# Layer 1 of a two-layer model: TensorE's steps put in another order by ranks and a re-measured planner clock

## The chip, the core and the metric

The kernel runs on one core of a Trainium2 chip. The metric is the device time of the whole program in microseconds; the kernel before has a median of 4030.48 us over three runs. TensorE is PE in the profile (PEld is its weight load), VectorE is DVE, ScalarE is ACT, GpSimd is POOL, and SyncE, which issues most transfers, is SP.

## The reference

The program computes two layers on x of shape (8, 1024, 256), all in float32. Layer 0 (attention, two expert layers and a Fourier block) is untouched here. Layer 1, cut to what matters:

```python
x = x + hla(layernorm(x), Wq, Wk, Wv, Wo)          # linear attention of higher order, 16 heads of 32, a scan over 1024 tokens
x = x + tanh(layernorm(x) @ W @ A1 @ A2 + bias)    # "ffn"
x = x + window(layernorm(x), Wqkv, bqkv, Wout, bout)  # softmax attention in windows of 128, 16 heads of 16
x = x + tanh(layernorm(x) @ W @ A1 @ A2 + bias)    # the same ffn

# one step of the scan in hla, G = 0.99
C_prev = G * C_QV
Gm   = G * Gm  + k[:, None] * (k @ C_prev)[None, :]
S_K  = G * S_K + k[:, None] * k[None, :]
C_QV = C_prev  + q[:, None] * v[None, :]
o    = q @ (S_K @ C_QV - Gm)
```

## The kernel before

Layer 1 handles a sequence (b, 0 to 7) in four pairs (i) of two chunks of 128 tokens; a chunk is c in the linear part and n in the window part. The scan is done by chunks: products of a chunk's queries and keys are masked and multiplied by tables of powers of 0.99, and a state of three 32x32 matrices a head passes from chunk to chunk.

The work is written as ten generators, each one a chain of steps that may interleave with the others:

- `enter` loads a pair of x (`x<-xb` on SP), eight pairs being resident at most.
- `linear_rows` ("lrows"): layernorm and transposes of a pair (helper `normed`, L1167), projections qt and kt (L1303), v (L1325), the masked products sk and sp (helper `head_products`, L1231 on PE, L1237 on DVE) and the transposes kw, dk, dq (L1343, L1358).
- `linear_chain` ("lchain"): the recurrence of a chunk: wt (L1251 and L1263), its transposes (L1392), ut, the new state (L1422, L1431, DVE L1440, POOL L1446), the products sr (L1231).
- `linear_out` ("lout"): the chunk's output (L1251, L1263), the projection with Wo (L1484) and the addition to x.
- `ffn` twice ("lffn" and "wffn"): layernorm, transposes, one product with the three matrices multiplied beforehand (L1189, L1198), tanh on ACT, addition on POOL (L1210).
- `window_rows` ("wrows"): layernorm, transposes, projections of k (L1510), q (L1530) and v (L1555, L1564), and on POOL the differences vd (L1582).
- `window_scores` ("wscores"): four banks of scores (L1599), the corner select and row maximum on DVE (L1613, L1615), exponentials on ACT (L1620).
- `window_columns` ("wcol"): transposes of the exponentials (L1641), copied by ACT (L1645) and, masked, by DVE (L1646).
- `window_out` ("wout"): products with v and vd (L1669), the denominators transposed (L1686, copied by ACT at L1692), the division on DVE (L1696), the projection (L1704).

A generator yields `step(cost, needs, acc, slots, tiles, dve)` before each piece of TensorE work. The class `Turns` keeps a planner's clock in units of about 0.108 us (a step of cost 16 is eight matmuls of 128x256, and takes 1.73 us in the trace). `ready` is the time at which the step's events and buffers are there by that clock; `run` takes the step with the earliest time and writes its instructions. TensorE executes in exactly that written order (`manual_schedule(engines={PE})`); DVE, ACT and POOL each have an in-order queue too, but the framework sorts theirs from the program as written. `use(engine, after, cost)` advances an engine's clock:

```python
start = max(self.engines[engine], after + 1.4)
self.engines[engine] = start + cost - 0.85
return start + cost + 0.6
```

and in `run` the choice among ready steps is

```python
change = 0.85 if request["tiles"][0] not in (None, self.tiles) else 0.0
start = at + change
if not self.ranks and self.engines["DVE"] < self.now + 15.0:
    change -= 0.05 * request["dve"]
key = (at + (0.0 if self.ranks else change), self.ranks.get(group, self.share.get(group, 0.0)), i)
```

`tiles` is how the step splits the 128x128 array: "whole", "rows" (four tiles of 32 rows), "columns" (four of 32 columns) or "halves". `self.ranks` is filled for layer 0 alone. PSUM has eight banks ("acc"); a bank is free again when the last reader of its step is done.

## Time and profile before

| what | value |
|---|---|
| median of 3 runs | 4030.48 us (4027.52 to 4034.27) |
| the profiled execution: its own time | 4030.48 us |
| the profiled execution: span, first to last instruction | 4028.5 us |
| mean granted TensorE clock | 0.974 of full speed |
| TensorE busy over the span | 3794.1 us (94%) |
| DVE, ACT, POOL busy over the span | 60%, 37%, 25% |
| layer 1, from 1687 us to the end | 2341.5 us, of which PE is busy 2223.93 us |

The busy time of PE is modelled, since its matmuls are pipelined; start times are recorded. All 31776 matmul records that layer 1 should have are in the trace, so that each can be assigned to the step that wrote it. Layer 1 has 1808 steps with TensorE work.

### The profile page before, as it was taken

The numbers are of one execution on the slowest core, as the hardware profiler recorded it, in microseconds if no ns is written. First come the engines' busy times: TensorE is split into PE (matmuls) and PEld (weight loads), VectorE is DVE, ScalarE is ACT, GpSimd is POOL, SyncE is SP. The second block draws the span as 40 slices with busy tenths as digits, with TensorE's granted clock in tenths as the row PEclk, the third lists the DMA queues.
The fourth block names the chain that finished last, engine by engine and source line by source line (L and its number), as shares of the span: only waits on it lengthen the run. The fifth ranks groups of instructions, "written<-read, shape, count | busy, mean of one in ns | idle before, by whom it ended". The sixth has DMA issues, their size and how long they took to land.

```text
span 4028.5 us, 92928 instructions
## 1 busy us (share of the span) xinstructions
PE 3794.1 (94%) x39176; PEld 2873.4 (71%) x39176; DVE 2409.9 (60%) x5653; ACT 1475.6 (37%) x4279; POOL 987.8 (25%) x1068
## 2 busy tenths in 40 slices
PE   8998999998699999999999999999999999999997
PEld 5665666676466666677778777777787777887775
DVE  5698036547765710156766666766766666667566
ACT  2322225322333212133534534434443445335335
POOL 1104463523242463211111111111211111111111
PEclk9998999999899999999999999999999999999999
DMA  4224444424243554200000000000000000000000
GB/s 137 85 69 142 114 122 107 107 69 121 65 106 86 134 130 108 58 2 7 7 12 7 13 7 7 12 7 7 12 7 12 7 7 12 13 5 5 7 5 9
DMA packets 164112, 196.43 MB, mean 49 GB/s; under 512 B 11248, under 2 KB 141296, under 8 KB 163696
## 3 DMA queue, kind: packets, MB, share of 16 engines
q1 hardware_dynamic: 139120, 156.92, 13.0%
q0 software_dynamic: 24576, 33.57, 5.0%
q8 instruction: 309, 5.06, 0.5%
q14 instruction: 107, 0.88, 0.1%
HBM read 131.60 MB, written 58.85 MB: 47 GB/s over the span
## 4 chain that ended last, share of the span: by engine, by line
PE 68%; DVE 15%; ACT 7%; issue 5%; POOL 4%; DMA 1%; SPq 0%; POOLq 0%; ACTq 0%; DVEq 0%
PE acc L489 10%; PE acc L517 9%; PE acc L1303 5%; PE acc L1263 5%; PE acc L1251 4%; PE acc L1231 4%; ACT w_ex L1620 3%; PE acc L1599 3%; PE acc L1484 2%; PE acc L1198 2%; PE acc L1669 2%; PE acc L1325 2%; DVE ln_st L270 2%; POOL ln_rs L273 2%; PE acc L595 2%
## 5 line engine op out<-in xcount | busy, mean ns | idle before, releaser
L273 POOL TENSOR_TENSOR ln_rs<-ln_rs,nhalf 128x2 f32<-128x2 f32 (+1 forms) x192 | 160.3, 836 | 1311.6 <-DVE ln_rs L272 1240.2
L489 PE MATMUL acc<-xgt,w1e 128*128 128x512 f32 x1024 | 460.1, 600 | 0.0
L1620 ACT ACTIVATE w_ex<-acc,w_nm 128x128 f32<-128x128 f32 x1024 | 362.8, 385 | 246.5 <-DVE w_nm L1615 240.6
L517 PE MATMUL acc<-w2e,ht 128*128 128x256 f32 x2048 | 452.3, 380 | 0.0
L517 PEld LDWEIGHTS acc<-w2e,ht 128*128 128x128 f32 x2048 | 385.6, 190 | 56.4 <-issue 5.9
L497 ACT ACTIVATE ht<-acc,b 128x512 f32<-128x512 f32 x256 | 174.2, 687 | 556.1 <-PE acc L489 555.8
L489 PEld LDWEIGHTS acc<-xgt,w1e 128*128 128x128 f32 x1024 | 192.9, 192 | 217.4 <-issue 212.0
L1303 PE MATMUL acc<-l_xt,hw 128*128 128x256 f32 x1024 | 240.0, 384 | 1.4 <-ACT l_xt L1174 0.8
L525 DVE SCALAR_TENSOR_TENSOR y<-acc,gate,gb 128x256 f32<-128x256 f32 x128 | 61.1, 478 | 293.5 <-PE acc L517 239.4
L270 DVE BATCH_NORM_STATS2 ln_st<-x 128x6 f32<-128x256 f32 x512 | 198.9, 409 | 55.6 <-POOL x L1210 36.1
L275 DVE TENSOR_SCALAR xn<-x,ln_mv,ln_rs 128x256 f32<-128x256 f32 x384 | 149.7, 434 | 137.7 <-POOL ln_rs L273 137.4
L1613 DVE COPY_PREDICATED acc<-consts,acc 128x256 f32<-128x256 int32 x512 | 193.0, 422 | 63.6 <-PE acc L1599 53.0
L1620 ACT ACTIVATION_READ_ACCUMULATOR w_ex<-acc,w_nm 128x1 f32 x1024 | 229.0, 224 | 0.0
L1446 POOL COPY state_bd<-state 32x384 f32<-32x384 f32 x224 | 112.6, 503 | 438.1 <-DVE state L1440 395.6
L1303 PEld LDWEIGHTS acc<-l_xt,hw 128*128 128x128 f32 x1024 | 191.2, 192 | 30.4 <-issue 2.4
L1646 DVE TENSOR_TENSOR w_pt<-acc,consts 128x512 f32<-128x512 f32 x256 | 167.1, 685 | 73.1 <-ACT w_pt L1645 71.3
L1237 DVE TENSOR_TENSOR sr<-acc,consts 128x512 f32<-128x512 f32 x256 | 158.9, 682 | 83.0 <-PE acc L1231 83.0
L512 POOL TENSOR_SCALAR gb<-b,gate 128x256 f32<-128x256 f32 x128 | 195.5, 1528 | 7.6 <-DVE index L433 7.5
L1615 DVE TENSOR_REDUCE w_nm<-acc 128x2 f32<-128x256 f32 x512 | 191.8, 416 | 0.0
L1237 DVE TENSOR_TENSOR sp<-acc,consts 128x512 f32<-128x512 f32 x256 | 158.7, 682 | 51.9 <-PE acc L1231 51.6
L1237 DVE TENSOR_TENSOR sk<-acc,consts 128x512 f32<-128x512 f32 x256 | 158.6, 682 | 37.3 <-PE acc L1231 37.3
L1645 ACT COPY w_pt<-acc 128x512 f32<-128x512 f32 x256 | 145.6, 620 | 94.0 <-PE acc L1641 82.9
(241 smaller groups left out, 7904.9 us busy)
## 6 DMA issues: line engine op xcount, KB each, us to landing
w1e<-in_W_dram SPq DMA_DIRECT2D x64, 512.0 KB
w2e<-in_W_dram SPq DMA_DIRECT2D x64, 512.0 KB
x<-in_x_dram SPq DMA_DIRECT2D x16, 512.0 KB
xa<-x SPq DMA_DIRECT2D x16, 512.0 KB
xna<-t_xn SPq DMA_DIRECT2D x16, 512.0 KB
x<-xa SPq DMA_DIRECT2D x16, 512.0 KB
gb<-g SPq DMA_DIRECT2D x32, 256.0 KB
xb<-x SPq DMA_DIRECT2D x16, 512.0 KB
```

What stands on the lines that cost most here:

```text
L270: nc.vector.bn_stats(st[:, i, :], src[:, i, :])
L273: nc.gpsimd.tensor_tensor(rs[:, :n], rs[:, :n], nhalf[:, :n], ALU.pow)
L489: nc.tensor.matmul(ps, w1e[:, k, (f % 4) * P : (f % 4 + 1) * P], xgt[:, k, :], start=k == 0, stop=k == 1,)
L497: nc.scalar.activation(h, ps, AF.Gelu_apprx_tanh, bias=b1[:, e * NT + f : e * NT + f + 1])
L512: nc.gpsimd.tensor_scalar(gb, r["b2", e], gate, None, ALU.mult)
L517: nc.tensor.matmul(ps[:, :D], ht[f][:, j * P : (j + 1) * P], r["w", e][2 + f // 4][:, f % 4, :], start=f == 0, stop=f == F // P - 1,)
L1237: nc.vector.tensor_tensor(dst, ps.rearrange("p (g t) -> p g t", t=P), bc4(const(mask)), ALU.mult)
L1263: nc.tensor.matmul(ps[32 * h : 32 * h + 32, g * P : (g + 1) * P], lhs(g, h), rhs[h][:, g, :], start=fresh and g == 0, stop=i == len(cols) - 1,
L1303: nc.tensor.matmul(ps[:, gi * 256 : (gi + 1) * 256], hw[:, k, g * 384 + col : g * 384 + col + P], xt[:, k, :], start=k == 0, stop=k == 1,)
L1613: nc.vector.copy_predicated(sc[:, :, 0, :], below, sc[:, :, 1, :])
L1615: nc.vector.tensor_reduce(nm, sc[:, :, 0, :], AX.X, ALU.max, negate=True)
L1620: nc.scalar.activation(ex[:, 2 * (j % 2) + e, :], sc[:, e, 0, :], AF.Exp, bias=nm[:, e : e + 1], accum_out=den[:, m, j, e : e + 1],)
```

## The change

No instruction of the computation is added or taken away; the planner's arithmetic is changed, and with it the order in which layer 1's steps are written. (1) Each step gets a `rank`, a number of units added to its key, so that it counts as later or, where negative, as earlier. (2) Leaving a "rows" step costs 2.1 units in the clock rather than 0.85. (3) The hand-over from TensorE to another engine costs 1.85 rather than 1.4 units (`use`), and between other engines 0 rather than 1.4 (`then`). (4) A few costs differ: POOL's power in the layernorm 7 rather than 10, a scores step 8 rather than 9, and vd counts from the end of the v additions. The core of the diff:

```diff
-    def use(self, engine, after, cost):
-        start = max(self.engines[engine], after + 1.4)
+    def use(self, engine, after, cost, lag=1.4):
+        start = max(self.engines[engine], after + lag)
         self.engines[engine] = start + cost - 0.85
         return start + cost + 0.6
...
-                    change = 0.85 if request["tiles"][0] not in (None, self.tiles) else 0.0
+                    change = 0.0
+                    if request["tiles"][0] not in (None, self.tiles):
+                        change = 2.1 if self.tiles in ("rows", "small") else 0.85
                     start = at + change
-                    if not self.ranks and self.engines["DVE"] < self.now + 15.0:
-                        change -= 0.05 * request["dve"]
+                    if not self.ranks:
+                        change += request["rank"]
+                        if self.engines["DVE"] < self.now + 15.0:
+                            change -= 0.05 * request["dve"]
...
-            done, use = turns.done, turns.use
+            done = turns.done
+            def use(engine, after, cost):
+                return turns.use(engine, after, cost, 1.85)
+            def then(engine, after, cost):
+                return turns.use(engine, after, cost, 0.0)
...  normed: layernorm and transposes
-                t = use("DVE", turns.now, 9.5)
-                t = use("POOL", t, 10)
-                done[tag, key, "n"] = use("DVE", t, 7)
-                t = yield step(4, [(tag, key, "n")], acc=1, slots=(tag,))
+                t = then("DVE", turns.now, 9.5)
+                t = then("POOL", t, 7)
+                done[tag, key, "n"] = then("DVE", t, 7)
+                t = yield step(4, [(tag, key, "n")], acc=1, slots=(tag,), rank=-1)
...
-                            t = yield step(9, needs, acc=4, slots=("w_ex", "w_ex"), dve=25)
+                            t = yield step(8, needs, acc=4, slots=("w_ex", "w_ex"), dve=25, rank=1)
...
-                                t_max = use("DVE", use("DVE", t, 4) - 1.4, 4)
+                                t_max = then("DVE", use("DVE", t, 4) - 1.4, 4)
...
-                        t = use("DVE", t, 4)
-                    acc_until(t)
+                        end = use("DVE", t, 4)
+                    acc_until(end)
...
-                            t = done["vd", b, m - 1] = use("POOL", t, 11)
+                            t = done["vd", b, m - 1] = then("POOL", end, 10)
```

The ranks, in units: `enter` 1; qt and kt 2; sk -11; dq -34; transposes of wt -2; ut -2; state -1; sr -2; projection with Wo 2; window k 5, q -29, v -64; scores 1; denominators -1; window projection 7; transposes of a layernorm -1; all other steps 0. The step with the smallest key is taken next. Its place on the clock is still `at` plus the real change of tiles, so that a rank alters the choice and not the lengths that the clock counts.

## The prediction

> **What bounds the kernel now.** I read the page first, then the stages by windows, then the timeline around single waits.

> ```profile
> span 4028.5 us, 92928 instructions
> PE 3794.1 (94%) x39176; PEld 2873.4 (71%) x39176; DVE 2409.9 (60%) x5653; ACT 1475.6 (37%) x4279; POOL 987.8 (25%) x1068
> ```

> TensorE sets the time; no other engine comes near. By windows, layer 1 is 2341.5 us, evenly loaded in the middle (a period of 577 us, two sequences) and thinner at its ends:

> ```profile
> core 0: us, PE busy (x) PEld busy (x) DVE busy (x) ACT busy (x) POOL busy (x), PEclk, DMA share, GB/s
> 1687.00:1787.00 100.00, 93.59 (x1333) 75.51 (x1337) 52.60 (x114) 32.25 (x80) 12.32 (x19) 0.93 0.04 14
> ...
> 2364.00:2941.00 577.00, 553.22 (x7950) 445.72 (x7952) 378.31 (x901) 249.46 (x831) 96.65 (x128) 0.98 0.03 9
> ...
> 3884.00:4028.50 144.50, 121.46 (x1478) 89.68 (x1476) 88.67 (x221) 65.32 (x242) 22.66 (x25) 0.94 0.03 9
> ```

> In the middle PE is idle for only 23.8 of 577 us. Busy time hides more, so I took start to start from the timeline, step by step. A kind of step has a usual length (the tenth percentile: a transpose of four blocks 0.44 us, a projection L1303 1.73, scores 1.08, a "rows" product 1.10). Over layer 1 the usual lengths make some 2042 of 2334.5 us, the half clock takes 45, and waits some 247. Two hundred and forty-seven is all that an order can win. A typical wait:

> ```profile
> 2673.00 1.16 PE L1251 MATMUL acc<-kt,state_bd 128*128 128x128 f32 x8
> 2674.09 1.08 PE L1263 MATMUL acc<-sk,v 128*32 128x128 f32 x32
> 2675.10 1.09 PE L1641 MATMUL acc<-consts,w_ex 128*128 128x128 f32 x8
> 2678.63 0.63 PE L1392 MATMUL acc<-consts,wt 128*128 128x128 f32 x4 [2.44 <-DVE sp L1237]
> ```

> ```profile
> 2675.40 1.25 DVE L272 TENSOR_SCALAR ln_rs<-ln_mv 128x2 f32<-128x2 f32 x1
> 2677.47 0.41 DVE L275 TENSOR_SCALAR xn<-x,ln_mv,ln_rs 128x256 f32<-128x256 f32 x1 [0.82 <-POOL ln_rs L273]
> 2677.80 2.48 DVE L1237 TENSOR_TENSOR sp<-acc,consts 128x512 f32<-128x512 f32 x4
> ```

> L1392 needs a PSUM bank that sp frees; sp stood behind a layernorm that waited for POOL. Three short steps stood between sp's products and L1392: too little work to cover the hand-over. Such waits are spread over many lines: by my count the scores take 41 us, L1641 25, L1669 20, the sk products 19, the sr products 19.

> **The change part by part.**

> *Instructions.* None is added. Comparing the built programs, layer 0 is identical on every engine, and layer 1 has the same first steps; PE's order differs from 1742.6 us on. SP's order is the same throughout, so every load and store keeps its place in that queue. A load now runs some 203 us of TensorE work ahead of its layernorm in the steady part, 290 before: far above the few us for which DVE waited on `x<-xb` (4.1 us in all). I cost the loads at nothing; were the lead gone, 24 later pairs would pay at most the 5 us that the planner itself allows. POOL's work moves with its steps and is within the counts below; it is busy 97 of 577 us. Semaphore waits change by some tens an engine; I cost them at nothing, since each is tied to a hand-over counted below.

> *Changes of tiling.* By how the array is really split (a scores step is a row step too), PE changes it 902 times before and 864 times after; leaving rows goes from 309 to 313. In the trace a step that is followed by another tiling is about 0.1 us longer (L1303 1.82 rather than 1.73; L1641 0.53 rather than 0.44). 38 fewer x 0.1 = -4 us. [...] I take -4.

> *Waits.* No trace shows the new order, so I bound it. For each waiting step I took the last TensorE step that must be over first, followed through the order of the DVE, ACT and POOL queues too, and summed the usual lengths between the two: the cover. Beside it stands the wait that this trace shows at such cover:

> | cover, us | steps before | mean wait before | steps after |
> |---|---|---|---|
> | under 0.5 | 43 | 1.15 | 7 |
> | 0.5 to 1 | 56 | 0.70 | 72 |
> | 1 to 1.5 | 107 | 0.28 | 59 |
> | 1.5 to 2 | 191 | 0.16 | 124 |
> | 2 to 3 | 278 | 0.16 | 262 |
> | 3 to 5 | 637 | 0.06 | 641 |
> | over 5 | 391 | 0.035 | 556 |

> Means times counts give 244 us before and 193 after: -50, the cautious end, since steps of unequal need share a row. The same table by kind of waiting step: -67. What is missing to a cover of 3 us sums to 779 us before and 540 after (-31%), to 2 us to 268 and 164 (-39%); of 247 that is -77 and -96. At the other end I took for each kind of hand-over the shortest lag seen (fifth percentile) and counted only what is missing to that: 436 places and 231 us before, 244 places and 102 us after: -129. There the transposes of the exponentials fall from 53 us in 27 places to 10 in 8, the window's first layernorm behind tanh and POOL's addition from 29 to 4, and vd (POOL L1582) from 12 to none. I take -90, between the last two and above the cautious end because the gains lie where lags are long.

> What comes late next: the Wo projection (L1484) behind the denominators' transposes (L1686), at 28 places with 1.1 us of cover for ACT's copy L1692; wt's transposes behind ACT's copy, 1.0 at some 30 places; sr behind ut on DVE, about 1.7 at 37. Those stay as waits and are in the counts.

> *Clock.* The windows view at three places of one period:

> ```profile
> core 0: us, PE busy (x) PEld busy (x) DVE busy (x) ACT busy (x) POOL busy (x), PEclk, DMA share, GB/s
> ...
> 2021.60:2028.40 6.80, 5.30 (x37) 4.01 (x40) 1.54 (x3) 3.70 (x12) 0.64 (x1) 0.51 0.01 2
> 2233.30:2240.10 6.80, 5.90 (x20) 4.25 (x18) 4.30 (x10) 2.22 (x4) 1.27 (x1) 0.51 0.00 0
> 2274.20:2281.00 6.80, 5.78 (x62) 4.85 (x62) 6.39 (x15) 2.91 (x16) 0.00 (x0) 0.51 0.01 2
> ```

> Each is 6.8 us at half clock, 3.4 us lost, and each follows a cluster of waits (before 2233.3 the four scattered starts of L1231, 3.0 us longer than usual). [...] The trace has them after waits in every period, so by the rows up to 31 us (three in each 577 us, and some more) could go. Between 0 and -31 I take -10: some clusters go, new ones may come.

> *End.* After the last linear projection 82.7 us of TensorE work remain, 71.3 before; at that end PE is idle 16% against 4% in the middle. 11.4 x 0.12 = +1.4, say +2.

> **Sum.** -4 - 90 - 10 + 2 = -102 us. The profiled execution took 4030.48 us (span 4028.5, 2.0 around it), which is also the median of the three runs: 4030.5 - 102 = 3928.5.

> **The rivals.**

> *A. Half the gain.* Queues of DVE and ACT add what the covers don't show: the cautious -50, no clock back, -4 and +2: 3978. For it: 72 steps in the row 0.5 to 1, more than before. Against: the counts follow those queues' order.

> *B. The waits only move.* The new order takes away covers that now work by luck; 247 us of waits remain, and -4 of tilings and +2 of the end give 4028, within measurement of no change. This is also the case in which the change does not do what it says: the planner's clock still errs by more than its ranks win. Against it: every row of the cover table under 0.5 and from 1 to 2 us is thinner.

> *C. Slower: ACT's copy of the denominators.* One mechanism, at one place: the Wo projection now follows L1686 at 28 places and needs the bank that L1692 frees on ACT, with 1.1 us of cover. On ACT a scores step is eight exponentials and eight reads (362.8 + 229.0 us over 128 steps = 4.6 us). If the copy stands behind a whole such block, each place waits about 4.6 + 0.9 - 1.1 = 4.4 us, 28 x 4.4 = 123 us, against a gain of 102: 4051. It decides from 102 / 28 = 3.6 us a place. For it: in the built ACT queue exponentials and two copies w_pt stand just ahead of the copy. Against: they belong to a step some 7 us earlier in PE's order and are mostly done, so I expect about 0.5 us a place.

> **How the numbers follow.** The main case (3928, itself from 3868 to 3961 by the ends -129 with the whole clock, and -67 with none) 0.68; A 0.22; B 0.05, of which half lies inside 0.2% (about 8 us, what a measurement of this kernel can tell from no change) and the rest is split; C 0.05. Faster: 0.68 + 0.22 + 0.01 = 0.91; same 0.03; slower 0.06. The range 3875 to 3990 takes in A and leaves out B, C, the upper part of A and the far end of the main case: about 2 in 10.

> **What would show it.** Right: from 1742 us on the period for one sequence falls from 288 to some 275 us; PE idle in layer 1 (2341.5 - 2223.9 = 117.6 us) falls to about 75; waits of L1641 and L1231 on w_ex and sp shrink; half-clock windows become fewer than three in two sequences; L1484's wait stays small. Wrong: layer 0 differs; the wait of L1484 on ACT L1692 grows to tens of us (C); idle stays above 110 us with other lines named (B); or the mean clock in the middle falls below 0.98.

## The result and the profile after

| | before | changed |
|---|---|---|
| median (4 runs each, the same chip) | 4032.38 us | 3979.30 us (3977.97 to 3979.71) |
| profiled execution: time, span | 4030.48, 4028.5 us | 3977.97, 3976.2 us |
| mean granted TensorE clock | 0.974 | 0.970 |

The ratio is 0.9869, with a 95% interval of 0.9852 to 0.9886: 53 us faster, inside the range, but only half of the 102 us that the sum gave. The changed kernel's lines in layer 1 stand 15 higher (L1231 is now L1246), those of the layernorm helper 6 (L275 is now L281). Its page begins:

```profile
span 3976.2 us, 92897 instructions
PE 3757.7 (95%) x39176; PEld 2880.5 (72%) x39176; DVE 2396.0 (60%) x5653; ACT 1468.7 (37%) x4279; POOL 987.1 (25%) x1068
```

The same three stretches by windows; the middle one is again two sequences:

```profile
core 0: us, PE busy (x) PEld busy (x) DVE busy (x) ACT busy (x) POOL busy (x), PEclk, DMA share, GB/s
1687.00:1787.00 100.00, 94.18 (x1439) 76.87 (x1440) 51.43 (x107) 28.90 (x63) 14.27 (x23) 0.95 0.03 10
2281.60:2841.30 559.70, 541.73 (x7944) 447.30 (x7944) 375.08 (x901) 247.68 (x830) 96.26 (x128) 0.98 0.03 10
3831.70:3976.20 144.50, 119.77 (x1331) 88.37 (x1329) 85.85 (x229) 73.39 (x290) 19.92 (x20) 0.90 0.03 10
```

A sequence takes 279.9 us instead of 288.5. The middle's idle time, 559.7 - 541.7 = 18.0 us, fell less than hoped (23.8 before), and the clock there did not rise.

The waits view of PE in layer 1 (line that waited, the bank or tile and its releaser: us in total, times, longest) tells why. Before:

```profile
PE acc L1231 <- DVE ut L1407: 13.2, 6, 2.5
PE acc L1198 <- ACT f_xt L1174: 10.8, 15, 1.5
PE acc L1167 <- DVE xn L275: 10.0, 2, 7.3
PE acc L1392 <- DVE sp L1237: 9.8, 4, 2.4
```

After:

```profile
PE acc L1246 <- DVE sp L1252: 56.3, 27, 2.6
PE acc L1182 <- DVE xn L281: 9.9, 2, 7.2
PE acc L1246 <- DVE ut L1422: 7.8, 12, 2.4
```

Before, many small entries; after, one large one (and the reverse on DVE: sp's masks waited 51.6 us for PE before, 0.9 after): `head_products` (L1246) waits for banks that the masks of sp (L1252) free. With the account of the prediction (start to start, each kind of step against its usual length), every matmul of layer 1 mapped in each kernel:

| layer 1, us | before | changed |
|---|---|---|
| usual lengths | 2037.7 | 2031.7 |
| waits | 247.4 | 189.0 |
| of which at the sk products | 19.2 | 82.9 |
| lost to half clock | 45.4 | 63.0 |

The rows add up to 2330.5 and 2283.7 us; from the first to the last matmul of layer 1 the traces have 2334.5 and 2282.4. So the account leaves some 5 us of the difference open, and figures of that size are at its edge.

All waits other than sk's fell from 228.2 to 106.1 us (scores 41.4 to 18.3, wcol's transposes 24.6 to 6.7, L1684 19.8 to 4.5). The sk products alone took back 64 us, at odd chunks and much the same in each sequence from the second on (but for the last chunk of all): 1.76 us at chunk 1, 2.9 to 3.4 at chunk 3, 3.64 at chunks 5 and 7. Here is chunk 5 of one sequence in the timeline of PE, DVE and POOL (start, length, line, operation, how often; the idle time before it and what ended it):

```profile
2627.91 1.17 PE L1246 MATMUL acc<-qt,kt 32*128 32x128 f32 x32
2629.94 1.88 PE L1340 MATMUL acc<-hw,l_xt 128*128 128x512 f32 x4
2631.76 0.48 PE L1246 MATMUL acc<-kt,qt 32*128 32x128 f32 x2
2634.81 1.76 PE L1246 MATMUL acc<-kt,qt 32*128 32x128 f32 x30 [2.57 <-DVE sp L1252]
```

```profile
2628.16 0.75 DVE L276 BATCH_NORM_STATS2 ln_st<-x 128x6 f32<-128x256 f32 x2 [2.32 <-POOL x L1225]
2630.59 0.73 DVE L281 TENSOR_SCALAR xn<-x,ln_mv,ln_rs 128x256 f32<-128x256 f32 x2 [0.67 <-POOL ln_rs L279]
2633.42 0.73 DVE L281 TENSOR_SCALAR xn<-x,ln_mv,ln_rs 128x256 f32<-128x256 f32 x2 [2.03 <-POOL ln_rs L279]
2634.07 2.48 DVE L1252 TENSOR_TENSOR sp<-acc,consts 128x512 f32<-128x512 f32 x4
```

```profile
2629.84 0.70 POOL L279 TENSOR_TENSOR ln_rs<-ln_rs,nhalf 128x2 f32<-128x2 f32 x1 [1.72 <-DVE ln_mv L277]
2631.47 1.26 POOL L1516 TENSOR_TENSOR x<-x,rows 128x512 f32<-128x512 f32 x1 [0.92 <-DVE ln_rs L278]
2632.68 0.70 POOL L279 TENSOR_TENSOR ln_rs<-ln_rs,nhalf 128x2 f32<-128x2 f32 x1
```

The sp products end at about 2629, but their masks start only at 2634.07. Ahead of them in DVE's queue the framework has put two layer norms: w_xt of the pair just finished (its statistics wait for POOL's L1225) and l_xt of the next pair. The second waits 2.03 us for its power on POOL, which stands behind the addition of bout (1.26 us). PE starts two sk matmuls and then waits for the third bank.

Each sequence now has three stretches in which the granted clock (PEclk, the last column but two) is half, after the waits at chunks 3, 5 and 7 (before, three in two sequences):

```profile
2281.60:2288.40 6.80, 6.44 (x77) 5.75 (x81) 4.59 (x8) 0.00 (x0) 0.00 (x0) 0.50 0.01 2
2356.60:2360.00 3.40, 3.40 (x40) 3.06 (x44) 2.35 (x4) 0.00 (x0) 0.00 (x0) 0.51 0.02 5
2428.30:2431.70 3.40, 3.40 (x40) 3.06 (x44) 2.37 (x4) 0.00 (x0) 0.00 (x0) 0.50 0.02 5
```

That is 13.6 us at half clock in a sequence, 6.8 lost, against 5.1 before: eight matmuls of L1266 took 2.08 us at half clock (from 2284.57 us) and 1.06 at full clock (from 2655.04).

### The profile page after: what moved, and what is told of

It reads as the page before. It is cut to its first block, busy times and chain, and to the rows that moved or that the text cites. A ratio compares the mean times of both kernels' runs of the same rounds, so it can differ in the third digit from the quotient of the medians.

```text
span 3976.2 us, 92897 instructions
## 1 busy us (share of the span) xinstructions
PE 3757.7 (95%) x39176; PEld 2880.5 (72%) x39176; DVE 2396.0 (60%) x5653; ACT 1468.7 (37%) x4279; POOL 987.1 (25%) x1068
## 4 chain that ended last, share of the span: by engine, by line
PE 77%; DVE 12%; POOL 5%; issue 3%; ACT 2%; DMA 1%; SPq 0%; POOLq 0%; ACTq 0%; DVEq 0%
PE acc L495 9%; PE acc L523 9%; PE acc L1318 6%; PE acc L1278 6%; PE acc L1266 5%; PE acc L1246 5%; PE acc L1614 3%; PE acc L1499 3%; PE acc L1656 3%; PE acc L1213 3%; PE acc L1684 3%; DVE ln_st L276 2%; POOL ln_rs L279 2%; PE acc L601 2%; DVE xn L281 2%
## 5 line engine op out<-in xcount | busy, mean ns | idle before, releaser
L281 DVE TENSOR_SCALAR xn<-x,ln_mv,ln_rs 128x256 f32<-128x256 f32 x384 | 140.7, 414 | 146.9 <-POOL ln_rs L279 146.9
L1252 DVE TENSOR_TENSOR sr<-acc,consts 128x512 f32<-128x512 f32 x256 | 158.9, 683 | 53.5 <-PE acc L1246 53.5
L1252 DVE TENSOR_TENSOR sk<-acc,consts 128x512 f32<-128x512 f32 x256 | 158.8, 683 | 26.6 <-PE acc L1246 26.6
L1246 PEld LDWEIGHTS acc<-kt,qt 32*128 32x128 f32 x2048 | 86.4, 199 | 116.7 <-DVE sp L1252 68.6
```

Of the source, the lines that this page charges most:

```text
L281: nc.vector.tensor_scalar(dst[:, i, :], src[:, i, :], mv[:, i, 0:1], rs[:, i : i + 1], ALU.subtract, ALU.mult)
L1246: nc.tensor.matmul(ps[:, g * P : (g + 1) * P], lhs[rs, g, :], rhs[rs, g, :], start=True, stop=True)
L1252: nc.vector.tensor_tensor(dst, ps.rearrange("p (g t) -> p g t", t=P), bc4(const(mask)), ALU.mult)
```

## The experiments

The kernel before was run beside each group of kernels: 4027.95 us in the first, 4034.04 in the second, 4026.79 in the third. Ratios are against that; medians of different groups can differ by some us for this alone.

### The two halves of the change, each alone

Ranks alone:

```diff
-    change = 2.1 if self.tiles in ("rows", "small") else 0.85
+    change = 0.85
...
     def use(engine, after, cost):
-        return turns.use(engine, after, cost, 1.85)
+        return turns.use(engine, after, cost)
...
     def then(engine, after, cost):
-        return turns.use(engine, after, cost, 0.0)
+        return turns.use(engine, after, cost)
```

The few changed costs, part (4) of the change, stay in this kernel and in all that follow but the one made from the kernel before; they were never taken alone, so "ranks" below means the ranks with them. The 1.4 and 0.85 of this expectation, and the 1.85 and 2.1 of later ones, are units of the planner's clock, about 0.108 us each, and not us.

> The changed kernel with the ranks and requests as they are, but with the old clock (1.4 us for every hand-over, 0.85 us for every change of tiling). Counted on its order: 278 places, 125 us short. Theory 1 (the ranks bring the gain): within 25 us of the changed kernel, 3970 to 4005 us. Theory 2 (the measured hand-overs bring it): at most a third of the gain, over 4010 us.

Measured: 3902.84 us, ratio 0.9695 (0.9675 to 0.9715). That is 76 us faster than the whole change: below the range of theory 1, and theory 2 is further off, since neither had the clock as a loss. Its hand-overs are a little shorter of cover than the changed kernel's, as counted (waits other than sk's 137.4 us, changed 106.1), but the sk products wait only 6.8 us and the half clock takes 25.3. The same chunk 5 on DVE:

```profile
2322.55 2.48 DVE L1252 TENSOR_TENSOR sk<-acc,consts 128x512 f32<-128x512 f32 x4
2324.95 0.74 DVE L1365 TENSOR_SCALAR dk<-acc,consts 128x512 f32<-128x512 f32 x1
2325.61 1.69 DVE L281 TENSOR_SCALAR xn<-x,ln_mv,ln_rs 128x256 f32<-128x256 f32 x2
2327.94 2.48 DVE L1252 TENSOR_TENSOR sp<-acc,consts 128x512 f32<-128x512 f32 x4 [0.65 <-PE acc L1246]
```

The powers and the addition of bout came earlier here; only one pair of xn is left between the two groups of masks, and the masks of sp wait for PE, not PE for them.

The clock alone:

```diff
     if not self.ranks:
-        change += request["rank"]
         if self.engines["DVE"] < self.now + 15.0:
```

> The changed kernel with the new clock, but without the ranks: a step's place in the order is due time and change of tiling alone, as before. Counted on its order of TensorE's steps, as in the prediction: 484 hand-overs closer than they are measured to need, 399 us short in all (before 436 and 231, changed 244 and 102). Theory 1 (the ranks are what brings the gain; the new clock alone lets the planner put steps close again): slower than before, between 4035 and 4110 us. Theory 2 (the measured hand-overs in the clock bring it): near the changed kernel, 3980 to 4000 us.

Measured: 4158.80 us, ratio 1.0325 (1.0308 to 1.0343): slower, as theory 1 had it, and by more than it gave. Waits are 316.7 us, and the half clock takes 102.1; I had priced no clock at all. The largest waits are the scores (68.2), the Wo projection (39.1) and the sk products (36.5).

### The layer norms ahead of the masks

In `head_products` the last mask is remembered, and `normed` queues its DVE instructions behind it. The edit ties instructions of DVE alone. In the traces TensorE's 1808 steps come in the changed kernel's order; on POOL the norms' powers follow to other places among the additions and copies.

```diff
+    masked = []
     def normed(tag, key, b, i, needs):
...
-        layernorm(xn, x, 2)
+        with tc.issue_after(masked[-1]) if masked else ExitStack():
+            layernorm(xn, x, 2)
...
-            nc.vector.tensor_tensor(
+            m = nc.vector.tensor_tensor(
                 dst, ps.rearrange("p (g t) -> p g t", t=P), bc4(const(mask)), ALU.mult
             )
+            masked[:] = [m.ins]
```

> The changed kernel with one thing more: the layer norms' instructions on VectorE are queued behind the masks of the pair whose products have just been made, so that they can't stand ahead of them. TensorE's order stays as it is. Theory 1 (the 64 us that the waits of the sk products took over come from two layer norms that stand ahead of the four masks on VectorE, the second of them waiting for POOL): those waits fall from 82.9 us to under 25, the half-clock windows behind them go with them (up to 31 of the 63 us lost), and the time is 3890 to 3925 us. Theory 2 (the four banks are asked for too soon after the first four products, whatever VectorE does in between; four masks of 0.62 us need 2.5 us): the waits stay above 50 us and the time is 3950 us or more. A third outcome: the layer norms come late instead, and TensorE waits for their outputs: over 3979 us.

Measured: 3853.50 us, ratio 0.9573 (0.9557 to 0.9589), 126 us under the changed kernel (119 by the ratios) and below even theory 1's range. The sk waits are 0.8 us, and the half clock takes 10.6 instead of 63.0. I had returned 31 of the 63 us to the clock at most; 52 came back. Waits elsewhere rose from 106.1 to 116.7, so the account gives -82 - 52 + 11 = -123 us. Chunk 5 of the same sequence on DVE:

```profile
2572.62 1.68 DVE L281 TENSOR_SCALAR xn<-x,ln_mv,ln_rs 128x256 f32<-128x256 f32 x2 [0.81 <-POOL ln_rs L279]
2574.22 2.47 DVE L1254 TENSOR_TENSOR sp<-acc,consts 128x512 f32<-128x512 f32 x4
```

The norm left in front is that of f_xt; those of w_xt and l_xt are made later, from 2587.96 and 2606.01 us on. The masks of sp start 0.25 us after sp's products end (2573.97), and the 32 sk matmuls follow on PE from 2576.72 us in one piece of 1.17 us. The waits view of PE in layer 1 no longer names the masks:

```profile
PE acc L1722 <- DVE w_ot L1714: 6.6, 3, 4.0
PE acc L1184 <- DVE xn L281: 6.6, 11, 2.7
PE acc L1248 <- DVE ut L1425: 3.3, 2, 2.4
```

The third outcome is there in small: the norms now come late at L1184, 6.6 us in 11 places. Two sequences by windows, and the end:

```profile
2247.00:2773.00 526.00, 525.39 (x7949) 433.98 (x7948) 381.96 (x901) 247.25 (x830) 96.23 (x128) 1.00 0.03 10
3704.00:3848.40 144.40, 118.36 (x1327) 86.72 (x1325) 87.32 (x235) 73.07 (x289) 21.91 (x22) 0.93 0.03 10
```

In the middle PE is idle 0.6 of 526 us, at full clock: there hardly anything is left for an order to win.

### POOL's part

The addition of bout is left out of the computation:

```diff
     x = xs[b, i]
-    nc.gpsimd.tensor_tensor(
-        x, x, row("bout").unsqueeze(1).to_broadcast([P, 2, D]), ALU.add
-    )
     then("POOL", turns.now, 12)
```

> The changed kernel without the addition of bout on POOL (left out of the result). Theory 1 in its POOL part (the second layer norm waits for its power on POOL, which stands behind this addition of 1.26 us): the sk waits lose about 1.26 us at some 27 places, -34 us, and some half-clock windows with them: 3925 to 3950 us. If only VectorE's own work in front of the masks counts (two norms of about 1.5 us each), POOL's addition is no part of it: within 10 us of the changed kernel, 3969 to 3989 us.

Measured: 3943.60 us, ratio 0.9792 (0.9775 to 0.9809). The time is where POOL's part put it, but by luck: the sum came together otherwise. At chunks 5 and 7 the wait fell from 3.64 to 2.42 us, by 1.22, and the gap ahead of the second xn from 2.03 to 0.81:

```profile
2623.69 0.73 DVE L281 TENSOR_SCALAR xn<-x,ln_mv,ln_rs 128x256 f32<-128x256 f32 x2 [0.81 <-POOL ln_rs L279]
2624.34 2.47 DVE L1252 TENSOR_TENSOR sp<-acc,consts 128x512 f32<-128x512 f32 x4
```

At chunk 3 it fell by some 0.5 us, and at chunk 1 it rose to 3.3, DVE's order being another there. So the sk waits lost 9.4 us (82.9 to 73.5) and not 34, and the half clock gave 23.7 (63.0 to 39.3).

### One norm or both

The queueing is limited to one tag:

```diff
-        with tc.issue_after(masked[-1]) if masked else ExitStack():
+        with tc.issue_after(masked[-1]) if masked and tag == "l_xt" else ExitStack():
```

> The changed kernel with only the next pair's layer norm (the one that makes l_xt) queued behind the masks; the other norm that stood ahead of them (w_xt, of the pair just finished) is free to. Theory 1 (it is the two norms together: the second waits for its power on POOL behind the first's and the bias addition, and at chunks 5 and 7 the masks start 2.8 us after the first norm is done): without one of them the sk waits fall from 82.9 us to under 30, and the time is 3865 to 3905 us. Theory 2 (the other norm alone is enough to hold the masks): waits over 50 us, 3940 us or more.

Measured: 3870.19 us, ratio 0.9617 (0.9599 to 0.9635); sk waits 17.8 us.

In the other, `"w_xt"` stands for `"l_xt"`:

> The same with only the norm that makes w_xt queued behind the masks, and l_xt's free to stand ahead of them. Theory 1 (the two together): waits at the sk products under 30 us, 3865 to 3905 us. Theory 2 (l_xt's norm alone is enough): over 50 us, 3940 us or more.

Measured: 3849.46 us, ratio 0.9562 (0.9544 to 0.9580); sk waits 0.9 us, and a sequence takes 261.3 us (262.9 with all norms queued). The waits of both bear out that it takes the two norms together. The second missed its range of time on the low side: I had not reckoned that w_xt's norm alone is all that has to move, and that l_xt and f_xt then aren't late (transposes of l_xt wait 1.5 us, 6.7 with all queued). It has the lowest median of all, by 4 us; the intervals of the two overlap, so the two are not told apart.

### Is the new clock a gain or a loss?

The same queueing of all norms was put into the kernel before, and into the parts of the change.

> The kernel before with the layer norms queued behind the masks. There the sk products waited 19.2 us, and the half-clock windows stand behind other waits too. Theory 1 (the norms ahead of the masks were a trap of the changed order alone): 4005 to 4030 us, at most 25 us less than before. Theory 2 (they cost any order as much): 3900 to 3950 us.

Measured: 3991.74 us, ratio 0.9893 (0.9876 to 0.9909), 42 us less than before: between the theories. The trap was there before too, but smaller, and at other lines than the sk products: `PE acc L1392 <- DVE sp L1237` (9.8 us) and `PE acc L1641 <- DVE sp L1237` (8.2) are gone from the waits view, L1231's waits for ut fell from 13.2 to 0.9, and late norms rose from 10.0 to 19.3.

> Ranks with the old clock, and the layer norms queued behind the masks. Without the queueing this order ran at 3902.8 us, with 6.8 us of waits at the sk products. Theory 1 (the hand-over counts hold for all that the norms don't disturb: this order is 125 us short where the changed kernel's is 102, and its usual lengths are 5 us longer): 3870 to 3890 us, some 30 us over the changed kernel with the same queueing (3853.5 us), so the new clock is worth that much once the norms are out of the way. Theory 2 (the new clock brings nothing to the ranks): 3845 to 3860 us. Theory 3 (the new clock costs by itself): under 3840 us.

Measured: 3888.65 us, ratio 0.9643 (0.9627 to 0.9659). Theory 1.

Two more kernels take one part of the clock each: first the new hand-overs with the old price of tiling, then the new price with the old hand-overs.

> Ranks, the new hand-overs (1.85 us and 0), the old price of a change of tiling (0.85 us everywhere), and the norms queued behind the masks. Counted: 109 us short, usual lengths 4 us longer than the changed kernel's. Theory 1 (the counts hold): 3858 to 3872 us. Theory 2 (prices of the changes of tiling are what the clock's part rests on): as ranks with the old clock, 3870 us or more.

Measured: 3861.14 us, ratio 0.9573 (0.9557 to 0.9589). Theory 1.

> Ranks, the old hand-over (1.4 us everywhere), the new price of a change of tiling (2.1 us out of rows and small tiles, else 0.85), and the norms queued behind the masks. Counted: 120 us short, usual lengths 5 us longer than the changed kernel's. Theory 1 (the counts hold): 3866 to 3885 us. Theory 2 (prices of the changes are what the clock's part rests on): near 3853 us, within 8.

Measured: 3884.89 us, ratio 0.9631 (0.9615 to 0.9647). That is the upper edge of theory 1, and 4 us from ranks alone, with overlapping intervals: the price of a change of tiling is not shown to bring anything. Nor is it beside the new hand-overs: the ratio is 0.9573 without it (e_lags_ln) and with it (e_ln_behind).

> The new clock without the ranks, and the norms queued behind the masks (without the queueing 4158.8 us, with 36.5 us of waits at the sk products). Theory 1 (without ranks this clock makes an order that is short by its own doing, 399 us by the counts against 231 before): the sk waits and a part of the half-clock loss go, 4080 to 4135 us, still 90 us or more over the kernel before with the same queueing (3991.7 us). Theory 2 (the norms ahead of the masks are why the clock alone was slow): 4010 us or less.

Measured: 4096.58 us, ratio 1.0179 (1.0159 to 1.0200). Theory 1: 62 us go with the norms, but 105 us over the kernel before with the same queueing remain. Why the new clock without ranks puts steps so close together stays open.

All in one table, medians in us:

| TensorE's order by | norms where the framework puts them | norms behind the masks |
|---|---|---|
| neither (before) | 4032.38 | 3991.74 |
| ranks alone | 3902.84 | 3888.65 |
| the new clock alone | 4158.80 | 4096.58 |
| ranks and new hand-overs | no run | 3861.14 |
| ranks and new prices of tiling | no run | 3884.89 |
| both (the change) | 3979.30 | 3853.50; only w_xt's norm 3849.46 |

And the account of layer 1 for some of them:

| us | usual lengths | waits | at sk | half clock |
|---|---|---|---|---|
| changed | 2031.7 | 189.0 | 82.9 | 63.0 |
| ranks alone | 2036.5 | 144.2 | 6.8 | 25.3 |
| changed, norms behind | 2031.7 | 117.5 | 0.8 | 10.6 |
| changed, w_xt's norm behind | 2031.7 | 102.5 | 0.9 | 20.6 |
| ranks alone, norms behind | 2036.5 | 134.8 | 0.6 | 20.4 |
| clock alone | 2047.9 | 316.7 | 36.5 | 102.1 |

## Why the prediction was right, and where it was not

Its direction and range held, and its likeliest number was 51 us too low. That the range held is in part luck: it was drawn wide for rival A, while no term had the 64 us lost at the sk products, the waits elsewhere fell by 32 more than the sum took, and the clock moved the other way. By its own steps:

- *Instructions at nothing.* Nothing in the runs speaks against it: PE, DVE, ACT and POOL have the same counts of instructions, and from 1687 us on the waits view of DVE names no load.
- *Tiling, -4.* The usual lengths fell by 6.0 us: of the right size, as far as the account can tell.
- *Waits, -90: mis-sized, measured -58.* The net hides two halves. Everywhere but at sk the waits fell by 122 us, so of the bounds the count by shortest lags (-129) came nearest, and my caution against it was misplaced. The sk products rose by 64. The step that failed is the cover: PE's work between a product and the step that needs its banks. It followed DVE's and POOL's queues to find which TensorE step comes last, but not how long those queues are busy themselves. From the end of the sp products to the sk products lay 2.75 us of PE's work (2629.01 to 2631.76); two norms, two powers and an addition took until 2634.07, 5.1 us, before the masks began. In the table this stands at "2 to 3 us, mean wait 0.16"; it cost up to 3.64. The prediction even showed one such wait (sp behind a norm that waited for POOL), and took it for one that thins out with the others.
- *Clock, -10: wrong in sign, measured +17.6.* "Some clusters go, new ones may come" was true, but the new ones came with the sk waits. Of the two ends between which the -10 was taken, -31 came from the half-clock windows of the trace; that nothing comes back, no trace had shown. In the steady part of the changed kernel, from 2000 to 3760 us, half clock followed the waits at chunks 3, 5 and 7 in every sequence, the longest idle gap of PE being 2.58 us; where the waits went (norms behind), those stretches went too. The loss fell from 63.0 to 10.6 us; from 45.4 before, that is 35, a little more than the 31 that the prediction held possible.
- *End, +2.* Of the last 144.5 us PE is idle in 24.7, before in 23.0; +1.7. But its clock is 0.90 instead of 0.94 there, some 6 us more, which is in the term above.

The rivals: A gives the measured number (3978), by luck of its sum (it had -50 for the waits and nothing for the clock; -58 and +17.6 were measured), and nearly the reason, that queues of DVE add what covers don't show. But the shortfall isn't spread: nearly all of it sits at one line, and is not a limit of the order, since moving the norms brings it back (sk waits 82.9 to 0.8 us). B is out: the waits did fall. Of C nothing came: `PE acc L1499 <- DVE ot L1490` stands at 0.5 us in one place.

Of what was to show it: the period fell to 279.9 us and not to 275; PE's idle time in layer 1 fell from 117.6 to 98.8 us and not to 75; half-clock stretches became six in two sequences rather than fewer than three; the middle's clock stayed at 0.98; the Wo projection's waits stayed small (13.4 to 8.6 us). Of the 98.8 us of idle time the waits view puts 56.3 down to sp's masks, and nothing else comes near. With the norms out of the way the change is worth some 130 us over the kernel before with the same queueing (ratios 0.9893 and 0.9573; 138 us by medians of different groups), most of it by the ranks (103, with the changed costs), and the new hand-overs bring some 28.

## What to carry to other kernels

Before an order of one engine is judged, follow each hand-over through the queue that it enters: sum the time of what stands ahead there, waits for a third engine included, and set that against the cover, rather than look only at the step that comes last. Work that is needed much later (w_xt's norm, made at 2630.59 and used by TensorE at 2658.18 us) may stand ahead of work that is needed at once; pinning just that one piece behind it brought here more than twice as much as the change of order. And test the parts of a change in each other's absence: the clock looked like a loss of 76 us beside the ranks and was a gain of about 30 once the norms were moved.

## What the hardware showed that was not expected

```profile
2552.00:2556.40 4.40, 2.93 (x35) 1.75 (x34) 3.59 (x9) 0.58 (x1) 0.69 (x1) 1.00 0.02 6
2556.40:2559.80 3.40, 3.40 (x48) 3.05 (x51) 2.25 (x4) 0.00 (x0) 0.00 (x0) 0.52 0.00 0
2623.00:2631.00 8.00, 6.53 (x187) 5.47 (x190) 6.58 (x12) 0.58 (x1) 1.28 (x3) 1.00 0.02 4
2692.00:2700.00 8.00, 6.53 (x190) 5.58 (x193) 6.58 (x12) 0.58 (x1) 1.28 (x3) 1.00 0.01 2
2759.00:2767.00 8.00, 5.65 (x169) 4.53 (x168) 7.19 (x15) 0.58 (x1) 0.69 (x1) 1.00 0.01 2
```

PE is idle for 1.47 us at chunk 3, and 3.4 us at half clock follow; after the same 1.47 us at chunks 5 and 7, and after 2.35 us at chunk 1, none follows. Cut at the grid, the four waits differ. "Work" is the sum over the matmuls of rows x columns x length of the moving operand, as a share of the median stretch of 3.41333 us in layer 1 of all thirteen traces:

| wait at | idle and work in the stretch where it starts | in the next one | half clock after |
|---|---|---|---|
| chunk 3 | 1.47 us, 31% | none (the half clock itself) | yes |
| chunk 5 | 1.08 us, 63% | 0.39 us, 63% | no |
| chunk 7 | 0.45 us, 83% | 1.02 us, 47% | no |
| chunk 1 | 1.60 us, 46% | 0.76 us, 58% | no |

The 1.47 us that fell into one stretch (chunk 3) left it with 31% of the work; the same 1.47 us spread over two left 63% in both (chunk 5), or 83% and 47% (chunk 7). In the thirteen traces 183 such stretches at full clock were followed by half clock in layer 1, and 161 of them had less than 40% of the median work; of the 8074 that were not followed, 19 had. The 40% is read from these traces, and no run varied the place on the grid alone. If the grid decides, the clock's share of a saved wait is hard to foresee: 1.22 us less at chunks 5 and 7 took away those stretches whole.
